# Two-layer graph kernel, first edge pass: ScalarE copies the sum of a group after the scaled relus of the next group of its batch

## The chip, the cores and the metric

The kernel runs on one core of a Trainium2 chip. The time is device time in microseconds (us) of one execution; a run's figure is a median over several executions. The engines named below are TensorE (PE, its weight loads PEld), VectorE (DVE), ScalarE (ACT), GpSimd (POOL) and SyncE (SP). Each runs its own queue of instructions in order; they wait for each other through semaphores. DMA transfers are issued from the queues of SP, ACT and POOL; all gathers of table rows by index are issued by POOL.

## What is computed

A graph with 30000 nodes of 128 features and 960000 edges sorted by destination. Layer 0 is two relational graph convolutions in a row, layer 1 is a gated convolution.

```python
def _rel_graph_conv(h, basis, coeff, bias, src, dst, etype, norm):
    W = jnp.einsum('rb,bdf->rdf', coeff, basis)          # 32 relations, 8 bases
    Hr = jnp.einsum('nd,rdf->nrf', h, W)
    msg = Hr[src, etype] * norm
    agg = jax.ops.segment_sum(msg, dst, num_segments=N)
    return agg + bias
...
h = jnp.maximum(_layernorm(x, axis=-1), 0.0)
x = x + layer0(h, ...)        # relu between its two convolutions
h = jnp.maximum(_layernorm(x, axis=-1), 0.0)
x = x + layer1(h, ...)        # sigmoid(k[dst] + q[src]) * v[src], summed by dst, mean of 4 types
```

## The kernel before

The edges are cut into tiles of 128 edges, three tiles make a group (384 edges, all of whose destinations lie in a window of 32 nodes), and five groups make a step. There are 2500 groups and 500 steps. Three edge passes follow each other: the first relational convolution, the second, and the gated layer. Each pass walks over all groups. A running sum `agg` (128 features by all nodes) stays in on-chip memory.

The change touches the body of the relational passes, and there only the order in the first one. What a step s of the first pass does, group by group (g = 0 to 4):

- POOL gathers the rows of x of the group's three tiles, three `DMA_INDIRECT` instructions (L118) into one buffer `hg` of a pool of seven. A gather into a buffer waits until the matmuls of the group that used it seven groups earlier are done.
- DVE takes the layer norm's statistics of the three gathered tiles (L410). Groups are normalised in two batches, which `BATCHES = {1: (0, 1), 4: (2, 3, 4)}` names: when group 1 has arrived, groups 0 and 1, and when group 4 has arrived, groups 2, 3 and 4. For a batch DVE combines the statistics (L415 to L420), ACT takes the square root (L422), DVE the reciprocal and the offset (L427, L429).
- DVE builds `sb` (L548): for each edge of the group its 8 basis coefficients, placed at its destination within the window.
- For each group of the batch ACT then runs three scaled relus in place on `hg` (L560), one for each tile; PE sums over the edges in `product`, three matmuls with 256 columns into a PSUM tile `pa` of a pool of three (L520), each of which waits for its own tile's relu; and ACT copies `pa` into `ab` (L531).
- After group 1, PE multiplies the previous step's `ab` by the eight bases into `pb` (`bases_out`, L478). PE then runs four small matmuls for the coefficients of a later step (L447), and in every second step two transposes that belong to finished nodes (L695, L696).
- At group 3, DVE adds the windows of an earlier step from `pb` into `agg` (`sums`, L351, five additions). They wait for the last `bases_out`, which writes the same PSUM tile. DVE's queue has them ahead of the statistics of group 4.

The order is written out by hand (`manual_schedule`): instructions stand in each engine's queue in the order in which the Python code makes them. In this pass the copy of a group stood at the end of `product`, so ACT's queue within a batch read: three relus, copy, three relus, copy, and in the longer batch once more. Between batches ACT also has the square roots, the copies and stores of finished nodes (L690, L699, L703) and the store of the coefficients for the second pass (L467).

The second pass runs the same code without statistics and relus and copies each group right after its product; the third pass has code of its own.

Of the kernel before, what the change touches and what calls it, by code (L numbers as in the profile page):

```python
# [72 lines left out]
def kernel(  # L73
# [43 lines left out]
    def gather(to, table, idx):  # L117
        return nc.gpsimd.indirect_dma_start(  # L118
            out=to, out_offset=None, in_=table,
            in_offset=bass.IndirectOffsetOnAxis(ap=idx, axis=0))  # L120
# [110 lines left out]
    def sorted_path():  # L231
# [7 lines left out]
        with ExitStack() as all_:  # L239
# [113 lines left out]
            def rel_body(table, weights, second):  # L353
# [21 lines left out]
                def body(bas, pos, hits, i, io, pool, ps, cp, iw, ic, beside):  # L375
# [5 lines left out]
                    def loads(k):  # L381
                        stage[k] = [stage_tile(io, "idx", src, I32, i, k)]
                        if second:
                            stage[k] += [stage_tile(io, "relc", reld, BF16, i, k),
                                         firsts(io, i, k)]
                        else:
                            dch = stage_tile(io, "dch", dst, I32, i, k)
                            fi = io.tile([TP, NGS], I32, name="fi")
                            n = i * NG + k * NGS
                            nc.sync.dma_start(fi, rows_of(first[n:n + NGS], TP))  # L390
                            stage[k] += [(dch, fi), firsts(io, i, k),
                                         stage_tile(io, "nrm", norm, F32, i, k,
                                                    4 * TQ - S * G)]

                    def positions(k):
                        dch, fi = stage[k][1]
                        relc = io.tile([TP, NTS], BF16, name="relc")
                        nc.vector.tensor_tensor(
                            relc.rearrange("p (g j) -> p g j", j=G),
                            dch.rearrange("p (g j) -> p g j", j=G),  # L400
                            fi.unsqueeze(2).to_broadcast([TP, NGS, G]), ALU.subtract)
                        stage[k][1] = relc
                        n = i * NQ + k
                        nc.scalar.dma_start(reld[:, n * NTS:(n + 1) * NTS], relc)
                        nc.vector.tensor_reduce(lo[:, n:n + 1], relc, AX.X, ALU.min)
                        nc.vector.tensor_reduce(hi[:, n:n + 1], relc, AX.X, ALU.max)

                    def statistics(st, hg):
                        for j in range(G):
                            nc.vector.bn_stats(st[:, j, :], hg[:, j, :])  # L410
# [86 lines left out]
                    for s in range(NS):  # L497
                        k = s // SB
                        if s % SB == 0:
                            if k + 1 < NQ:  # L500
                                loads(k + 1)
                        idx, relc, start = stage[k][:3]
                        if s + 2 < NS:
                            (kept if second else types)(s + 2)
                        z = s // A
                        if s % A == 0:
                            ab[z] = pool.tile([P, B, Z, W], F32, name="ab")
                        t0 = s % SB * S * G
                        nc.vector.tensor_tensor(
                            hits, iw[:TP].unsqueeze(1).to_broadcast([TP, S * G, W]),  # L510
                            relc[:, t0:t0 + S * G].unsqueeze(2).to_broadcast([TP, S * G, W]),
                            ALU.is_equal)
                        if not second and s % SB == SB - 1 and k + 1 < NQ:
                            positions(k + 1)
                        held = {}

                        def product(g, hg, rows, sb):
                            pa = ps.tile([P, B, W], F32, name="pa", bufs=3)
                            for j in range(G):
                                made = nc.tensor.matmul(  # L520
                                    pa.rearrange("p b w -> p (b w)"), lhsT=hg[:, j, :],
                                    rhs=sb[:, j].rearrange("p b w -> p (b w)"),
                                    start=(j == 0), stop=(j == G - 1))
                                if j == 0 and second:
                                    for other in rows[1:]:
                                        tc.add_manual_dep(
                                            made.ins, other.ins.name,
                                            mybir.DependencyInfo(mybir.DependencyClass.Sync,
                                                                 mybir.DependencyReason.DATA),
                                            reason="all rows of a group first")  # L530
                            nc.scalar.copy(ab[z][:, :, s % A * S + g, :], pa)  # L531

                        for g in range(S):
                            t0 = (s % SB * S + g) * G
                            hg = pool.tile([TP, G, D], F32, name="hg", bufs=5 if second else 7)
                            rows = [gather(hg[:, j, :], table, idx[:, t0 + j:t0 + j + 1])
                                    for j in range(G)]
                            ready = BATCHES.get(g)
                            if not second:
                                if g in (0, 2):  # L540
                                    st = pool.tile([TP, 3 * G, 6], F32, name="st")
                                at = (g if g < 2 else g - 2) * G
                                statistics(st[:, at:at + G], hg)
                                if ready:
                                    both, rs = spread(st, at + G)
                            sb = pool.tile([TP, G, B, W], F32, name="sb", bufs=4)
                            of = slice(g * G, (g + 1) * G)
                            nc.vector.tensor_mul(  # L548
                                sb, hits[:, of, :].unsqueeze(2).to_broadcast([TP, G, B, W]),
                                ce[s][:, of, :].unsqueeze(3).to_broadcast([TP, G, B, W]))  # L550
                            held[g] = hg, rows, sb
                            if second:
                                product(g, *held[g])
                            elif ready:
                                off = shifted(both, rs, at + G)
                                for q, one in enumerate(ready):
                                    for j in range(G):
                                        n = q * G + j
                                        mine = held[one][0][:, j, :]
                                        nc.scalar.activation(mine, mine, AF.Relu,  # L560
                                                             scale=rs[:, n:n + 1],
                                                             bias=off[:, n:n + 1])
                                    product(one, *held[one])
                            if g == 1 and z and s % A == 0:
                                bases_out(z - 1)
                            if g == 2 and not second and s + 1 < NS:
                                coefficients(s + 1)
                            if g == 3 and not second:
                                keep(s)
                                if s + 2 < NS:  # L570
                                    onehot(s + 2)
                            if second and z and s % 2 and g in (1, 3):
                                sums(s - 3 + g // 2)
                            if not second and g == 3 and s > 1:
                                sums(s - 2)
                            if s == NS - 1 and g == 2 and second:
                                bases_out(NS // A - 1, 0)
                            if s == NS - 1 and g == 4:
                                sums(NS - 2)
                            if g == 3 and s % SB == 1:  # L580
                                base[k] = bases(start, DVE)
                            beside(s * S + g)
# [552 lines left out]
```

## Time and profile before

| what | value |
|---|---|
| median of 10 runs | 36218.07 us (36176.04 to 36253.35) |
| the profiled execution's own time | 36205.21 us |
| its span | 36203.3 us |
| TensorE's mean granted clock in it | 0.663 |
| busy: PE, PEld | 21389.7 us (59%), 16826.8 us (46%) |
| busy: POOL | 21247.4 us (59%) |
| busy: DVE | 13768.0 us (38%) |
| busy: ACT | 6808.2 us (19%) |
| HBM traffic | 2603.78 MB read, 256.02 MB written |

Times on the page are microseconds unless marked ns. A row of a group of instructions names the line, the engine, the operation, the tile written and the tiles read, the count, then the busy time and the mean duration in ns, then how long the engine sat idle just before these instructions and what ended most of that idle time ("issue": nothing that the profile shows; "remote": a semaphore was raised by something that the profile can't name). In the timeline each row is a start, a duration, the engine and the instruction, with the idle time before it in brackets. The granted clock is TensorE's share of full speed: 1.0 or 0.5 at any moment, and a mean over a stretch.

No engine is busy for more than 59% of the span, and the span splits by pass: the first lasts to about 14160 us, the second to about 24890 us, the third to the end. In the stretch from 40 to 14180 us PE is busy for 7897.22 us, DVE for 5892.23, ACT for 4324.49 and POOL for 7072.25 us, at a granted clock of 0.68.

### The profile page before, as it was taken

How to read it: one execution, taken by the hardware profiler on the slowest of the kernel's cores; microseconds unless marked ns; L12 is line 12 of the kernel's file. 1: busy time of each engine (PE TensorE's matmuls, PEld its weight loads, DVE VectorE, ACT ScalarE, POOL GpSimd, SP SyncE). 2: the span in 40 equal slices, each digit the busy share in tenths (PEclk: the TensorE clock that was granted, in tenths of full speed). 3: DMA queues.
4: the chain of work that ended last, by engine and by line, in shares of the span. 5: the costliest groups of instructions: out<-in, count | busy, mean ns of one | idle time of the engine just before them, and what ended most of it. 6: DMA issues, size and time to landing. Idle time of an engine off the chain costs nothing. (4 is left out here: it accounts for less than half of the span.)

```text
span 36203.3 us, 289281 instructions
## 1 busy us (share of the span) xinstructions
PE 21389.7 (59%) x79371; PEld 16826.8 (46%) x79371; DVE 13768.0 (38%) x36932; ACT 6808.2 (19%) x18026; POOL 21247.4 (59%) x22513
## 2 busy tenths in 40 slices
PE   5555555555555556666666666666555655555565
PEld 3344444434444444444444444444555555555555
DVE  4444444444444443333333333333333333333333
ACT  3333323333333332111111111111111111111111
POOL 5445445445545445666666666666666666666666
PEclk7666666666666666778888788886555555555555
DMA  2112112112212212222222222223444444444444
GB/s 59 50 50 58 49 49 58 50 49 56 52 50 56 51 50 53 67 67 67 67 67 67 66 68 67 67 67 97 127 126 126 126 126 126 126 126 126 126 126 122
DMA packets 2002776, 2880.25 MB, mean 80 GB/s; under 512 B 708374, under 2 KB 1391247, under 8 KB 2001167
## 3 DMA queue, kind: packets, MB, share of 16 engines
q0 software_dynamic: 840000, 1967.52, 20.2%
q1 hardware_dynamic: 749240, 638.42, 6.1%
q10 hardware_dynamic: 411927, 255.71, 2.7%
q8 instruction: 662, 10.85, 0.1%
q14 instruction: 947, 7.76, 0.1%
HBM read 2603.78 MB, written 256.02 MB: 79 GB/s over the span
## 5 line engine op out<-in xcount | busy, mean ns | idle before, releaser
L520 PE MATMUL pa<-sb,hg 128*128 128x256 f32 x30000 | 10718.9, 514 | 8362.7 <-ACT hg L560 5080.0
L520 PEld LDWEIGHTS pa<-sb,hg 128*128 128x128 f32 x30000 | 7235.7, 256 | 11601.9 <-ACT hg L560 6101.5
L118 POOL DMA_INDIRECT hg<-in_x,idx x7500 | 7081.3, 944 | 7034.4 <-PE pa L520 4792.5
L118 POOL DMA_INDIRECT qv<-qvtab,qi x7500 | 7088.7, 945 | 4208.8 <-issue 2093.4
L118 POOL DMA_INDIRECT hg<-h,idx x7500 | 7075.4, 943 | 3647.9 <-issue 2125.6
L633 PE MATMUL po<-sel,msg 128*128 128x32 f32 x15000 | 3454.7, 386 | 4547.7 <-DVE msg L631 4163.6
L633 PEld LDWEIGHTS po<-sel,msg 128*128 128x128 f32 x15000 | 3427.9, 328 | 4835.3 <-DVE msg L631 4312.6
L531 ACT COPY ab<-pa 128x256 f32<-128x256 f32 x5000 | 1848.2, 373 | 14169.4 <-PE pa L520 6391.9
L659 DVE TENSOR_TENSOR pk<-pk,qv 128x384 f32<-128x384 f32 x2500 | 1405.8, 562 | 7001.4 <-remote 5534.1
L622 PE MATMUL pk<-kw,oh 128*128 128x128 f32 x15000 | 3997.2, 439 | 11.6 <-DMA kw<-ktab 11.6
L622 PEld LDWEIGHTS pk<-kw,oh 128*128 128x128 f32 x15000 | 3476.6, 331 | 11.8 <-issue 11.8
L560 ACT ACTIVATE hg<-hg,off,rs 128x128 f32<-128x128 f32 x7500 | 3155.3, 485 | 656.6 <-DVE off L429 491.0
L478 PE MATMUL pb<-ab,bas 128*128 128x160 f32 (+1 forms) x12080 | 2629.0, 376 | 406.9 <-issue 205.6
L351 DVE TENSOR_TENSOR agg<-agg,pb 128x32 f32 x5000 | 936.3, 187 | 4611.7 <-remote 3543.3
L660 ACT ACTIVATE pk<-pk 128x384 f32<-128x384 f32 x2500 | 1187.5, 475 | 7797.0 <-DVE pk L659 4720.0
L478 PEld LDWEIGHTS pb<-ab,bas 128*128 128x128 f32 x12080 | 2171.2, 214 | 876.2 <-issue 376.9
L548 DVE TENSOR_TENSOR sb<-cp,ce 128x768 f32<-128x768 f32 x2500 | 2319.5, 948 | 624.2 <-remote 423.5
L548 DVE TENSOR_TENSOR sb<-hits,ce 128x768 f32<-128x768 f32 x2500 | 2362.5, 945 | 59.3 <-PE pa L520 52.6
L410 DVE BATCH_NORM_STATS2 st<-hg 128x6 f32<-128x128 f32 x7500 | 1674.7, 278 | 167.3 <-issue 167.1
L427 DVE RECIPROCAL rs<-rs 128x6 f32<-128x6 f32 x1000 | 197.9, 198 | 3305.6 <-ACT rs L422 1206.4
L750 PE MATMUL bank<-wall,hT 128*120 128x512 f32 x1518 | 927.9, 728 | 746.8 <-ACT hT L746 316.0
L631 DVE TENSOR_TENSOR msg<-pk,qv 128x384 f32<-128x384 f32 x2500 | 1365.8, 546 | 0.0
(86 smaller groups left out, 7978.4 us busy)
## 6 DMA issues: line engine op xcount, KB each, us to landing
kb<-kcode SPq DMA_DIRECT2D x500, 480.0 KB
kw<-ktab SPq DMA_DIRECT2D x2500, 64.0 KB
er<-in_et_row SPq DMA_DIRECT2D x500, 256.0 KB
hg<-in_x,idx POOLq DMA_INDIRECT x7500
hg<-h,idx POOLq DMA_INDIRECT x7500
qvtab<-qvt ACTq DMA_DIRECT2D x250, 480.0 KB
qv<-qvtab,qi POOLq DMA_INDIRECT x7500
ktab<-kt ACTq DMA_DIRECT2D x253, 240.0 KB
```

The lines of the kernel that those rows point to most:

```text
L118: return nc.gpsimd.indirect_dma_start(out=to, out_offset=None, in_=table, in_offset=bass.IndirectOffsetOnAxis(ap=idx, axis=0))
L410: nc.vector.bn_stats(st[:, j, :], hg[:, j, :])
L478: nc.tensor.matmul(po[z][:, of].rearrange("p s w -> p (s w)"), lhsT=bas[:, b, :], rhs=ab[z][:, b, of].rearrange("p s w -> p (s w)"), start ...
L520: made = nc.tensor.matmul(pa.rearrange("p b w -> p (b w)"), lhsT=hg[:, j, :], rhs=sb[:, j].rearrange("p b w -> p (b w)"), start=(j == 0), ...
L531: nc.scalar.copy(ab[z][:, :, s % A * S + g, :], pa)
L548: nc.vector.tensor_mul(sb, hits[:, of, :].unsqueeze(2).to_broadcast([TP, G, B, W]), ce[s][:, of, :].unsqueeze(3).to_broadcast([TP, G, B, W]))
L560: nc.scalar.activation(mine, mine, AF.Relu, scale=rs[:, n:n + 1], bias=off[:, n:n + 1])
L622: nc.tensor.matmul(pk[n][:, j, :], lhsT=oh[n // S][:, n % S, j * TP:(j + 1) * TP], rhs=kw[n], start=True, stop=True)
L631: nc.vector.tensor_mul(msg, pk[n], qv[n][:, :, 1, :])
L633: nc.tensor.matmul(po[s][:, g, :], lhsT=msg[:, j, :], rhs=sel[s][:, g * G + j, :], start=(j == 0), stop=(j == G - 1))
L659: nc.vector.tensor_add(pk[n], pk[n], qv[n][:, :, 0, :])
L660: nc.scalar.activation(pk[n], pk[n], AF.Sigmoid)
```

## The change

The copy is taken out of `product`, which now returns its PSUM tile, and a new function `copied` issues it. The second pass calls it right after `product`, as before. In the first pass the copy of a group is issued after the relus and the product of the next group of the batch, and the copy of the batch's last group at the end. ACT's queue in the batch (0, 1) becomes: relus of 0, relus of 1, copy of 0, copy of 1. In the batch (2, 3, 4): relus of 2, relus of 3, copy of 2, relus of 4, copy of 3, copy of 4. Apart from a few separate wait instructions every engine issues the same work as before, and only ACT issues it in another order.

```diff
@@ in body, second and first pass
                                             reason="all rows of a group first")
-                            nc.scalar.copy(ab[z][:, :, s % A * S + g, :], pa)
+                            return pa
+
+                        def copied(g, pa):
+                            nc.scalar.copy(ab[z][:, :, s % A * S + g, :], pa)
...
                             if second:
-                                product(g, *held[g])
+                                copied(g, product(g, *held[g]))
                             elif ready:
...
                                         nc.scalar.activation(mine, mine, AF.Relu,
                                                              scale=rs[:, n:n + 1],
                                                              bias=off[:, n:n + 1])
-                                    product(one, *held[one])
+                                    made = product(one, *held[one])
+                                    if q:
+                                        copied(*last)
+                                    last = one, made
+                                copied(*last)
```

## The prediction

> **What bounds the kernel now.** I first asked which engine is full. None is: the page gives POOL and PE 59% each. So I took the pass that the change touches, the first, and read there who waits for whom (the list of waits of the stretch from 2000 to 12000 us, about 355 of the 500 steps; columns: waiter, releaser, us in total, times, longest).
>
> ```profile
> POOL hg L118 <- PE pa L520: 3393.3, 952, 12.4
> ...
> DVE agg L351 <- remote: 2482.2, 250, 12.5
> ...
> DVE agg L351 <- PE pb L478: 404.2, 66, 7.4
> ```
>
> POOL waits for buffers that PE frees: 3393.3 us over 355 steps, 9.6 us a step, nearly all in one long wait. DVE's additions L351 wait too: 250 times for a semaphore whose raiser the profile can't name, 66 times for PE's `pb`. How these belong together is seen in the timeline. Here are two steps in a row.
>
> ```profile
> 6003.13 2.93 PE L520 MATMUL pa<-sb,hg 128*128 128x256 f32 x6 [5.19 <-ACT hg L560]
> ...
> 6006.34 0.94 POOL L118 DMA_INDIRECT hg<-in_x,idx  x1 [8.69 <-PE pa L520]
> ...
> 6016.32 2.34 PE L478 MATMUL pb<-ab,bas 128*128 128x160 f32 x16
> ...
> 6023.97 0.95 POOL L118 DMA_INDIRECT hg<-in_x,idx  x1 [0.30 <-issue]
> ...
> 6027.91 1.08 DVE L351 TENSOR_TENSOR agg<-agg,pb 128x32 f32 x5 [10.92 <-remote]
> 6028.91 0.67 DVE L410 BATCH_NORM_STATS2 st<-hg 128x6 f32<-128x128 f32 x3
> ...
> 6031.51 1.26 ACT L560 ACTIVATE hg<-hg,off,rs 128x128 f32<-128x128 f32 x3 [0.83 <-DVE off L429]
> ...
> 6035.26 0.94 POOL L118 DMA_INDIRECT hg<-in_x,idx  x1 [10.34 <-PE pa L520]
> ...
> 6035.84 2.93 PE L520 MATMUL pa<-sb,hg 128*128 128x256 f32 x6 [0.85 <-ACT hg L560]
> ...
> 6043.55 0.30 ACT L422 ACTIVATE rs<-both,eps 128x6 f32<-128x6 f32 x1 [0.42 <-issue]
> ...
> 6044.85 2.93 PE L520 MATMUL pa<-sb,hg 128*128 128x256 f32 x6 [2.30 <-ACT rs L422]
> ...
> 6048.06 0.94 POOL L118 DMA_INDIRECT hg<-in_x,idx  x1 [1.79 <-issue]
> ...
> 6051.35 3.69 PE L478 MATMUL pb<-ab,bas 128*128 128x160 f32 x16
> ...
> 6055.31 1.08 DVE L351 TENSOR_TENSOR agg<-agg,pb 128x32 f32 x5 [7.37 <-PE pb L478]
> ...
> 6062.66 0.94 POOL L118 DMA_INDIRECT hg<-in_x,idx  x1 [7.39 <-PE pa L520]
> ```
>
> A step is a closed loop. POOL is released by the product of group 2 (6006.34) and issues a burst of fifteen gathers. Then it must wait for the next step's product of group 2. That one needs the statistics of group 4, and those stand in DVE's queue behind L351. From L351 to the next burst is a fixed tail: 6027.91 to 6035.26 and 6055.31 to 6062.66, 7.35 us both times. So the period is the time from the burst's first gather to L351, plus 7.35: 21.57 + 7.35 = 28.92 in the first step, 20.05 + 7.35 = 27.40 in the second.
>
> The odd thing is what ends the wait of L351. In the first step `pb` is finished by its records at 6018.66, yet L351 starts at 6027.91, 9.25 us later and 2.99 us after the last gather's end. In the second, PE is slower (matmuls of 2.93 where others take 1.56), `pb` ends at 6055.04, and L351 follows 0.27 us behind. The step in which PE was late is the shorter one. I took both marks from the timeline for all 495 steps with complete neighbours and sorted them by how long the tenth gather of the burst was held up (the one at 6048.06, which needs the product of group 0):
>
> - held up by 1.3 us or more: 139 steps, mean period 25.98 us, L351 in the median 19.7 us after the burst's start
> - less: 356 steps, mean 29.16 us, L351 at 21.5 us. Among them 202 with no hold-up at all (under 0.15 us): mean 29.14 us, L351 between 21.1 and 21.6 us nine times in ten, whether `pb` ended 12.3 or 16 us after the burst's start
> - all: 28.26 us, times 500 = 14130 us, the length of the pass.
>
> I can't name the mechanism; as a rule of this trace: a `pb` that ends early is seen by DVE only when the burst is over and 2 to 3 us more; a `pb` that ends 17 us or later after the burst's start is mostly seen soon. The fast steps are those in which PE is late.
>
> **The change, part by part.** *Relus move ahead of copies.* Before, product 3 waits for relus that wait for the copy of 2: PE stands idle 0.85 us between two products of a batch (row 6035.84). After, the relus of group 3 end 2 x 1.26 = 2.5 us after the first relu of group 2, while product 2 takes 2.93, so product 3 follows at once. In the batch of three two gaps of 0.85 vanish: 1.7 us earlier end of product 4. In the batch of two one gap: 0.85. *Copies move back.* The copy of 2 (0.37) comes up to 1.3 us later, those of 3 and 4 earlier. A product needs the copy of three groups before (three `pa` tiles); product 0 of the next step needs that of group 2, over by then: nothing, hidden behind products 3 and 4. Without that cover it would be one copy, 0.37 us a batch. *What stands behind on ACT.* L422 of the next batch comes behind the copy of 4: 1.7 us earlier, so product 0 starts at 6043.15 in place of 6044.85, and the tenth gather, held up 1.49 beyond the usual 0.30, is no longer held up. Stores and the two transposes' relu move forward with it. *Tail.* Product 2, which frees the next burst, has its relus first in both orders: 7.35 us stay. No instruction, DMA or byte is added.
>
> So PE ends `pb` at least 1.7 + 0.85 = 2.55 us earlier, and bursts run without the hold-up. By the rows, that takes the 139 short steps into the class of the 202. The price: bounds are 0 (they stay short) and 139 x (29.14 - 25.98) = 439 us. The 202 hold somewhat many of the steps with the longer tail of 9.2 us (48 of 202; all: 101 of 495), 0.04 x 1.85 = 0.07 us, and their steps with the earliest `pb` have L351 at 21.2 in place of 21.5. I put the new mean at 29.0 us: (29.0 - 28.26) x 500 = +370 us. On the profiled execution's 36205.2 (span 36203.3 and 1.9 around it; 13 below the median, which I neglect) that is 36575 us. Upper end: every step at 21.6 + 7.35 + 0.2 x 1.85 = 29.32, +530, 36735. Lower end of this case: half the short steps survive, +185, 36390. The second pass and the third keep their order: 0.
>
> The granted clock comes in: 0.68 in this pass, as PE falls to half speed in its idle stretches. Closing the gaps makes the stretch of three products 8.8 us without a break, so it may turn fast sooner, which moves `pb` still further into the class where nothing is gained. The Trainium skill, "TensorE: Matmul & The Clock Gate", Part 1, says that about 3.4 us of sustained activity release the half clock. By that page alone the third product and all behind it would take 1.56 in place of 2.93, and if `pb` set L351, as an estimate 3 x 1.37 us more would come off in each of the 139 steps, some 570 us in all. By the rows of the 202 steps it is worth nothing.
>
> **Rivals.** *L351 follows `pb` (faster).* If the short steps are short for another reason, and there `pb` goes on setting L351, each gains 2.55 us: 139 x 2.55 = 355, 35850 us; with half of them 36030. For it: the 66 waits that name `pb`. Against it: in 250 others an earlier `pb` brought nothing. It decides from the point where L351 starts less than 21 us after the burst's start though the tenth gather isn't held up. *No change.* The short steps' early release hangs on something that the order doesn't touch, and PE's gain lies in the wait of L351 as it does in the 250: 36205, within 70. For it: steps that alternate, the second kind (with the two transposes) being long whatever PE does. Against: among the others, the steps without the transposes, 116 (of 244) without a hold-up of 1.3 us have a mean of 29.15. *The order does not take effect,* since a copy held back blocks a `pa` tile: excluded by the three tiles, as above; it would show as a wait of L520 for the copy and give 36205 plus at most 0.37 x 1000 = 36575.
>
> **How the numbers follow.** Longer steps, 36390 to 36735: 0.68, likeliest 36575. Faster rival: 0.21. No change: 0.09, copies that block: 0.02 (slower). A measurement of this kernel tells 0.2% (72 us) from nothing. So faster 0.21, same 0.09, slower 0.70. The range goes from 36050, which takes in no change and the weakest part of the faster rival, to 36740.
>
> **What would show it.** Right: products of a batch without the 0.85 us in front; the tenth gather held up in few steps; L351's waits named "remote" near 500 for the pass and those for `pb` almost gone; the pass some 370 us longer, the tail still 7.35 us; passes two and three as they were. Wrong: L351 earlier than 21 us in many steps with an unbroken burst, or a pass of under 14100 us.

## The result, and the profile after

The changed kernel takes 36438.62 us (8 runs, 36427.5 to 36445.99) where the kernel before took 36223.49 (28 runs, 36176.04 to 36262.96): a ratio of 1.0059, 95% interval 1.0051 to 1.0068. It is slower by 215 us; the forecast was 357 us (36575 against 36218). The profiled execution has a span of 36443.5 us, 240 more than before (the two profiled executions lie 18 us below and 7 above the medians).

That is one kind of chip. Later runs fell on chips on which the kernel before takes 30528 to 30544 us, and there the same change is faster by 7.4% (run a2 below). Each later run is compared with the kernel before, timed beside it on the same chip; the text names the chips by that time, "36.2 ms chip" and "30.5 ms chips".

Where did the 240 us of span come from? The last gather of the first pass ends at 14376.6 us, before at 14117.9: 259 us later. From there to the end it is 22066.9 us, before 22085.4. So it is the first pass alone: a mean step of 28.79 us in place of 28.26. The waits of the stretch from 2000 to 12000 us, as shown of before (waiter, releaser, us in total, times, longest):

```profile
DVE agg L351 <- remote: 4340.0, 340, 14.5
POOL hg L118 <- PE pa L520: 3598.0, 526, 13.5
```

In some 347 steps L351 now waits 340 times for a raise of a semaphore that the profile can't name, 12.8 us each (before 250 times, 9.9 us). The line that named `pb` L478 as its releaser is gone. One step in the timeline (start, duration, engine and instruction, idle time before it):

```profile
3003.57 6.51 PE L520 MATMUL pa<-sb,hg 128*128 128x256 f32 x18 [15.10 <-ACT hg L563]
...
3006.53 0.37 ACT L534 COPY ab<-pa 128x256 f32<-128x256 f32 x1 [1.09 <-PE pa L520]
...
3006.77 0.94 POOL L118 DMA_INDIRECT hg<-in_x,idx  x1 [10.26 <-PE pa L520]
...
3011.91 2.86 PE L520 MATMUL pa<-sb,hg 128*128 128x256 f32 x12 [1.83 <-issue]
...
3014.60 2.34 PE L478 MATMUL pb<-ab,bas 128*128 128x160 f32 x16
...
3018.01 0.94 POOL L118 DMA_INDIRECT hg<-in_x,idx  x1 [0.30 <-issue]
...
3024.26 0.94 POOL L118 DMA_INDIRECT hg<-in_x,idx  x1 [0.30 <-issue]
3028.01 1.08 DVE L351 TENSOR_TENSOR agg<-agg,pb 128x32 f32 x5 [13.01 <-remote]
```

The products of a batch are now one row: 18 matmuls without a gap, then 12. The tenth gather (3018.01) starts 0.30 us behind the ninth, so the burst runs unbroken in 18.42 us. `pb` is written by 3016.94 in the records. Yet L351 starts at 3028.01, 11 us later and 2.8 us after the end of the last gather (3025.20). PE's semaphore shows it directly: its raises for `pb`, for L447 and for the two transposes, which the records end between 3016.94 and 3017.99, all come between 3027.92 and 3028.08. Over the stretch from 100 to 8000 us the lateness builds up within a burst: of the 784 matmuls that make a raise and end in a burst's first 2 us, 781 have one recorded within 0.15 us, of those that end 6 to 8 us into it 28 in 100, of those at 10 to 12 us 2 in 100; between bursts (26 to 28 us) all 431 have one. The raises of DVE and ACT aren't late here: none of 7765 and 4388 comes 1 us behind its instruction. Over 495 steps L351 starts 21.2 us after the burst's start (21.1 to 21.5 in eight steps of ten), while `pb` ends at 10.3 in the median (before at 16.4).

### The profile page after: what moved, and what is told of

It is laid out like the page before. It is cut to its first block, busy times and chain, and to the rows that moved or that the text cites. A ratio compares the mean times of both kernels' runs of the same rounds, so it can differ in the third digit from the quotient of the medians.

```text
span 36443.5 us, 289276 instructions
## 1 busy us (share of the span) xinstructions
PE 19842.9 (54%) x79371; PEld 16404.8 (45%) x79371; DVE 13772.8 (38%) x36932; ACT 6749.4 (19%) x18026; POOL 21267.6 (58%) x22513
## 5 line engine op out<-in xcount | busy, mean ns | idle before, releaser
L520 PE MATMUL pa<-sb,hg 128*128 128x256 f32 x30000 | 9307.8, 471 | 10131.0 <-ACT hg L563 7338.1
L520 PEld LDWEIGHTS pa<-sb,hg 128*128 128x128 f32 x30000 | 6971.6, 241 | 12267.0 <-ACT hg L563 7503.5
L351 DVE TENSOR_TENSOR agg<-agg,pb 128x32 f32 x5000 | 936.4, 187 | 6438.4 <-remote 6236.0
L563 ACT ACTIVATE hg<-hg,off,rs 128x128 f32<-128x128 f32 x7500 | 3047.3, 482 | 659.8 <-DVE off L429 526.0
L478 PE MATMUL pb<-ab,bas 128*128 128x160 f32 (+1 forms) x12080 | 2476.3, 360 | 322.3 <-ACT ab L534 198.4
L478 PEld LDWEIGHTS pb<-ab,bas 128*128 128x128 f32 x12080 | 2009.1, 199 | 757.4 <-issue 274.5
L422 ACT ACTIVATE rs<-both,eps 128x6 f32<-128x6 f32 x1000 | 301.9, 302 | 7317.6 <-DVE both L420 7156.4
L740 DVE BATCH_NORM_STATS2 st<-bank 120x6 f32<-120x128 f32 x253 | 75.5, 299 | 3303.8 <-remote 1862.3
```

The costliest lines, as they stand in the source:

```text
L478: nc.tensor.matmul(po[z][:, of].rearrange("p s w -> p (s w)"), lhsT=bas[:, b, :], rhs=ab[z][:, b, of].rearrange("p s w -> p (s w)"), start ...
L520: made = nc.tensor.matmul(pa.rearrange("p b w -> p (b w)"), lhsT=hg[:, j, :], rhs=sb[:, j].rearrange("p b w -> p (b w)"), start=(j == 0), ...
L563: nc.scalar.activation(mine, mine, AF.Relu, scale=rs[:, n:n + 1], bias=off[:, n:n + 1])
```

## The experiments

**Loop or not: the additions moved.** First I tested that the step's loop runs through L351 at all. In e1 the changed kernel issues the additions two groups earlier, ahead of the `bases_out` that writes their tile; e2 does the same to the kernel before. Both on the 36.2 ms chip.

```diff
+                            if not second and g == 1 and s > 1:
+                                sums(s - 2)
                             if g == 1 and z and s % A == 0:
                                 bases_out(z - 1)
...
-                            if not second and g == 3 and s > 1:
-                                sums(s - 2)
```

> The additions L351 of step s-2 are issued at group 1, ahead of the bases_out of step s-1, so that they need only the bases_out of the step before. Theory A (the step's loop runs through L351, which waits for a semaphore of PE that is raised late; the burst of gathers, 18.4 us, is then the next bound): the first pass falls from 28.8 us a step to between 19 and 25 us, 500 x (28.8 - 19 to 25) = 1900 to 4900 us, a total of 31500 to 34500. Rival B (another wait for the same late semaphore, the one-hot sums of the next step, hits L509, which wait for L447, takes its place in DVE's queue): 28 to 29 us a step, total 36100 to 36500.

> The same early additions with the copies in the order of before. Theory A: L351 out of the loop, the order of the copies still costs 1.7 us in the chain from the statistics to product 0 and 0.85 us between products, so this is equal to e1_sums_early where POOL is the bound, or up to 500 x 2.5 = 1250 us slower than it; the order of the change is then the better one. Rival B (the loop goes on through a late semaphore): this one stays ahead of e1_sums_early by 200 to 250 us, as before is ahead of the changed kernel.

e1: 33012.21 us, ratio 0.9113 (0.9098 to 0.9128), 21.9 us a step. e2: 33092.08, ratio 0.9135 (0.912 to 0.9151). Theory A holds for both, and rival B of either run is out: over 3100 us were the price of one wait, in either order of the copies. With L351 out of the loop the change is worth 80 us on this chip too, where alone it loses 215. The waits of e1 (2000 to 10000 us):

```profile
ACT ab L534 <- remote: 1299.0, 241, 8.9
...
DVE agg L707 <- remote: 1070.8, 127, 11.2
DVE hits L509 <- remote: 768.5, 92, 10.6
...
POOL hg L118 <- remote: 623.4, 189, 3.7
```

L351 no longer has a line of size. Raises that nobody can be named for now hold the copies, the finished nodes (L707), the one-hot sums and POOL itself. POOL's waits for these and for products (716.1 us on L520) come to 3.7 us a step, and a step takes 21.9 us in place of the 18.7 of fifteen gathers.

**PE made late by work.** The prediction had read that the short steps are those in which PE is late. So I made PE late, on the same chip.

```diff
                             if g == 1 and z and s % A == 0:
-                                bases_out(z - 1)
+                                for _ in range(1 if second else 4):
+                                    bases_out(z - 1)
```

> The changed kernel with bases_out done four times in a row in each step of the first pass (the same result each time), 3 x 2.34 = 7.0 us of PE work more in each step. Theory A (steps are short when PE ends pb late, whatever held it up): pb ends about 11.0 + 7.0 = 18.0 us after the start of the burst, L351 follows at once in the steps without transposes (243 of 489), which become 18.1 + 7.7 = 25.8 us, and perhaps in the others: total 36440 - 700 to 1500 = 34900 to 35750, faster with more work. Rival B (before's short steps were short because the burst itself had a hole at the tenth gather): L351 stays at 21.2 us, total 36440 within 70. Rival C (PE's work counts): 7 us more in each step, total up to 39900.

38929.8 us, ratio 1.0746 (1.0728 to 1.0764): 5.0 us a step slower than the changed kernel. Theory A falls, and so does rival B, which had the time unchanged; rival C, that PE's work counts, comes nearest (5.0 us of its 7). The timeline of the burst that begins at 3004.22 and whose last gather ends at 3022.66 shows more:

```profile
3011.99 5.20 PE L478 MATMUL pb<-ab,bas 128*128 128x160 f32 x36
...
3018.30 0.43 PE L478 MATMUL pb<-ab,bas 128*128 128x160 f32 x2 [1.10 <-issue]
...
3020.39 0.43 PE L478 MATMUL pb<-ab,bas 128*128 128x160 f32 x1 [1.67 <-issue]
...
3021.11 0.90 PE L478 MATMUL pb<-ab,bas 128*128 128x160 f32 x2 [0.29 <-issue]
...
3023.22 0.43 PE L478 MATMUL pb<-ab,bas 128*128 128x160 f32 x1 [1.21 <-issue]
...
3025.35 5.02 PE L478 MATMUL pb<-ab,bas 128*128 128x160 f32 x19 [0.26 <-issue]
...
3030.48 1.07 DVE L351 TENSOR_TENSOR agg<-agg,pb 128x32 f32 x5 [18.09 <-PE pb L478]
```

36 matmul records follow each other in 5.2 us, the next nine take from 3018.30 to 3025.09, and at 3025.35, again 2.7 us after the last gather's end, PE runs on at its pace. So it is not only the raise that is late: here PE's work itself comes almost to a halt until the gathers are over. The Trainium skill, "TensorE: Matmul & The Clock Gate", "Architectural detail", gives TensorE's queue 64 entries. 36 matmuls with their weight loads are 72 instructions; whether a full queue is what stops PE, no run here shows.

**A pause in the burst, by a wait.** In e4 the last three gathers of a burst wait for the `bases_out` of the step before.

```diff
+                            if not second and g == 3 and s:
+                                tc.add_manual_dep(
+                                    rows[0].ins, ab["made"].ins.name,
...
```

> The changed kernel with the gathers of group 3 of each step (the last three of a burst) made to wait for the bases_out of the step before, so that POOL pauses after twelve gathers until PE's semaphore is raised. Theory A (the raise comes some 2.7 us after POOL has gone quiet, and not at a fixed time): POOL's twelfth gather ends 14.6 us after the burst's start, the raise comes at about 17.4, L351 starts there, next burst 7.4 us later: 25 us a step, total about 34500 (34000 to 35200). Rival (the raise comes at a fixed time of the step, 21.2 us, whatever POOL does): POOL pauses until then, L351 stays at 21.2, and the three last gathers follow beside the tail: total 36440 within 100. A third (the raise waits for the landing of the whole burst for another reason): POOL pauses longer than 10 us, total above 36600.

37240.95 us, ratio 1.0281 (1.0263 to 1.0298): the third case by its time, but the timeline shows the pause longer for another reason.

```profile
3019.24 0.95 POOL L118 DMA_INDIRECT hg<-in_x,idx  x1 [0.30 <-issue]
...
3022.67 0.37 ACT L535 COPY ab<-pa 128x256 f32<-128x256 f32 x1 [3.50 <-remote]
...
3029.32 2.34 PE L478 MATMUL pb<-ab,bas 128*128 128x160 f32 x16
...
3032.42 0.95 POOL L118 DMA_INDIRECT hg<-in_x,idx  x1 [12.24 <-issue]
```

POOL is quiet from 3020.19. The raise that the copy waits for comes 2.4 us later; what follows (square root, relus, two products, `pb`) then takes until 3031.66 with every raise in time. So the raises come out once POOL is quiet, but the awaited `pb` had not even begun; the edit put a chain of 9 us into the loop. It settles nothing on the size of the gain.

**The parts of the change, and holes of fixed length.** The next runs fell on a 30.5 ms chip, which I had not reckoned with. e5 keeps the new order in the batch of three alone, e6 in the batch of two alone; e7 and e7s put memsets on POOL ahead of the tenth gather.

```diff
 e5 (e6: the other way round)
+                                    if len(ready) != 3:
+                                        copied(one, made)
+                                        continue
...
 e7 (e7s: once)
+                            if not second and g == 2:
+                                idle = pool.tile([TP, 1024], F32, name="idle", bufs=1)
+                                for _ in range(3):
+                                    nc.gpsimd.memset(idle, 0.0)
```

> The change in the batch of three alone (relus of 2, 3, copy of 2, relus of 4, copies of 3, 4); the batch of two as before. L422 and product 0 come 1.7 us earlier, so the tenth gather isn't held up; pb 1.7 us earlier. Theory H (what made before's short steps short is the hole in the burst, the tenth gather held up by 1.3 us or more): nearly all steps long, like the changed kernel: 36350 to 36500. Rival P (it is the time at which PE ends pb): pb ends about 15.4 us after the burst's start in the steps that had it at 17.1, also all long: the same. Both fall if this kernel stays at 36220; then it is the batch of two that costs.

> The change in the batch of two alone (relus of 0, 1, copies of 0, 1); the batch of three as before, so the tenth gather stays held up by 1.49 us where it was, and pb ends 0.85 us earlier. Theory H (the hole in the burst makes the short steps): about as many short steps as before, 36150 to 36300. Rival P (the time at which PE ends pb decides): pb at 16.3 in place of 17.1 us after the burst's start falls among the steps with L351 at 21.2, long: 36380 to 36500.

> The changed kernel with three memsets of 128x1024 on POOL before the tenth gather of each burst: a hole of some 3 us (the trace will tell) in which POOL issues no gather; all else as in the changed kernel, pb done by the records 11 us after the burst's start. Theory H (a pause of POOL lets PE's late semaphores out): L351 starts at about 14 us, the next burst follows when POOL is done with this one, some 22 us a step, total about 33000 (32500 to 34500): idling POOL makes the kernel faster. Rival P (the raise is late when PE is early, whatever POOL does): L351 stays at the burst's end plus 2.7, which moves by the hole: 36440 + 500 x 3 = 37900.

> The same with one memset, a hole of some 1 us, less than the 1.49 us by which before's short steps held the tenth gather up. Theory H, if a short pause is enough: as many or more short steps than before, below 36220. Theory H, if the pause must last as long as the time from a burst's end to L351 (2.7 us): 36440 + 500 x 1 = 36940. Rival P: 36940 too.

| run | time, us | before on this chip | ratio (interval) | mean step, first pass |
|---|---|---|---|---|
| e5, batch of three | 28501.03 | 30543.62 | 0.9334 (0.9317 to 0.9352) | 19.39 us |
| e6, batch of two | 29987.58 | 30543.62 | 0.9823 (0.9804 to 0.9841) | 22.36 us |
| e7, hole of 2.84 us | 29675.01 | 30543.62 | 0.972 (0.9699 to 0.9742) | 21.74 us |
| e7s, hole of 0.83 us | 28652.89 | 30543.62 | 0.9386 (0.9365 to 0.9407) | 19.69 us |

All four expectations were stated for the other kind of chip, and none can be judged by its times; e5, e6 and e7s weren't run on that kind, so theory H for the parts of the change and for a short hole stays untested there. What the traces show instead is why this chip is faster. I compared the raises of PE's semaphore recorded from 100 to 8000 us with the end of PE's latest matmul that makes one: in the kernel before on the 36.2 ms chip 20% come over 1 us late, in the changed kernel 23%, in e1 52%. (The expectation of a2 below has 36 and more; these counts don't give that for the first two.) In these four runs none of 6351 to 7339 does. The traces differ in the number of raises too: the changed kernel's has 3731 for 4932 matmuls that make one, e5's 7339 for 7341, so the shares on the first chip hold only for the raises that are recorded. The gathers are alike on both (0.94 us, 0.30 us apart), and so are the DMA packets of 4096 bytes that they move (median 201 ns before, 202 in e5, over the whole execution). The other two passes gain too, 22085 us there and 18818 us here (e6), with the code untouched.

**The change where nothing is late.** So the changed kernel was run once more, with e8 beside it: e1 in which the one-hot sums read their index row from SBUF rather than from the PSUM tile that L447 writes.

```diff
+                    iw = iw if second else irow
```

> The changed kernel once more, since the kernel before took 36223 us on the chip of the first runs and 30544 us on that of e5 to e7s, where no raise of PE's semaphore in the trace is over 1 us late (36 in 100 and more were around there). Theory L (the loss comes from PE's late raises alone, and these belong to the chip): where the kernel before takes about 30540, this takes what e5_late_in_three took or less, 28150 to 28510, ratio 0.92 to 0.935; where it takes about 36220, it takes 36440 again, ratio 1.006. Rival (the change costs by itself, whatever the raises do): a ratio over 1 on both kinds of chip.

> e1_sums_early, and in the first pass the one-hot sums L509 read the index row from SBUF and not from the PSUM tile that L447 writes, so that they wait for no raise of PE. Theory A (each wait of DVE for a late raise adds to the loop): where the kernel before takes about 36220, less than the 33012 of e1_sums_early, 31500 to 32900. Rival (POOL's wait for product or the copies' waits set the pace there): 33012 within 100. Where the kernel before takes about 30540, POOL's gathers are the bound at 18.72 us a step, and it is equal to the changed kernel on that chip within 150 us, 28100 to 28500.

It fell on a chip of the second kind. The changed kernel: 28235.89 us against 30527.86, ratio 0.9257 (0.9236 to 0.9277). e8: 28287.4, ratio 0.9273 (0.9252 to 0.9293), 51 us behind it. Theory L holds: no raise of 7512 is late, and the sign turns. The timeline and the waits (2000 to 9000 us) of the changed kernel there:

```profile
3000.53 2.34 PE L478 MATMUL pb<-ab,bas 128*128 128x160 f32 x16
...
3002.97 1.08 DVE L351 TENSOR_TENSOR agg<-agg,pb 128x32 f32 x5 [1.34 <-PE pb L478]
```

```profile
DVE agg L351 <- PE pb L478: 492.3, 278, 3.7
POOL hg L118 <- PE pa L520: 165.6, 523, 2.3
```

L351 follows `pb` by 0.1 us in the midst of the gathers, nothing is "remote", and POOL waits for products 165.6 us in some 370 steps, 0.45 us a step. A step is 18.86 us, fifteen gathers at 1.248 are 18.72: POOL is the bound. For the kernel before on this chip I have no trace; 30527.86 less the 18802 that the other passes take (28233.5 - 9431.8, the end of the first pass in a2) leaves 11726 us, 23.4 us a step. So what the change removes is worth 4.6 us a step there, and e5 and e6 say in which batch: the batch of three alone brings 2043 us, the batch of two alone 556. The holes of e7 and e7s cost there what they last: 29675 - 28236 = 1439 us, 2.88 us a step, and 417, 0.83 a step (across two chips whose kernel before differs by 16 us).

**The hole and the row again.** The last two runs are e8 and e7 once more, on a chip of the first kind (the kernel before 36637.96 us).

> The same kernel as e8_own_index_row, for a chip on which PE's raises are late. Where the kernel before takes about 36220: theory A (each of DVE's waits for a late raise adds to the loop) 31500 to 32900; rival (the copies' and POOL's own waits for late raises set the pace, 21.9 us a step in e1_sums_early) 33012 within 100. Where it takes about 30530: 28290 within 50 again.

> The same kernel as e7_hole_three_memsets, for a chip on which PE's raises are late; its hole is 2.84 us beyond the usual 0.30. Where the kernel before takes about 36220: theory H (a pause of POOL lets PE's late raises out) L351 at about 14 us after the burst's start, 21.7 us a step as where nothing is late, the first pass 10900 us, total 32500 to 34500; rival P (raises come 2.7 us after the last gather of a burst, whatever pause it had) L351 at 24, 31.6 us a step, total about 37900. Where it takes about 30530: 29675 within 50 again.

e7b: 33626.07 us, ratio 0.9179 (0.9164 to 0.9194). With POOL kept from gathering for 3 us in each step the changed kernel is 8% faster than the kernel before where raises are late, as theory H had it (32500 to 34500), and the rival's 37900 is out; without the hole it was 0.6% slower than before on the 36.2 ms chip (it wasn't run on this one). L351 moves to 14.3 us after the burst's start in the median, a step takes 22.7 us. In the timeline:

```profile
3028.30 2.34 PE L478 MATMUL pb<-ab,bas 128*128 128x160 f32 x16
...
3030.38 0.95 POOL L118 DMA_INDIRECT hg<-in_x,idx  x1 [0.31 <-issue]
...
3031.32 3.00 POOL L542 MEMSET idle<- 128x1024 f32 x3
...
3033.41 1.08 DVE L351 TENSOR_TENSOR agg<-agg,pb 128x32 f32 x5 [4.71 <-remote]
...
3034.47 0.95 POOL L118 DMA_INDIRECT hg<-in_x,idx  x1 [0.15 <-issue]
```

`pb` ends by its records at 3030.64, POOL's last gather before the hole at 3031.33, and the raises of `pb`, L447 and the transposes come together from 3033.32 to 3033.48, 2.0 us into the hole. The memsets keep POOL busy all that time: the raises wait for a pause in the gathers, not in POOL's work as such.

e8b: 33343.23 us, ratio 0.9102 (0.9087 to 0.9117), against 0.9113 (0.9098 to 0.9128) for e1: the same, by ratios, as the kernel before differs by 1.1% between the two. The rival holds; one DVE wait less brings nothing that can be measured.

## Why the prediction was right, and where it wasn't

*Products close up, the tenth gather runs free.* As forecast: one row for a batch, and the tenth gather held up by 1.3 us or more in 3 of 489 steps, before in 139 of 495. In those three L351 still starts early, 10.6 us after the burst's start in the median.

*`pb` earlier, L351 not.* Forecast was `pb` at least 2.55 us earlier with nothing gained. It ends at 10.3 us after the burst's start, 6.1 us earlier in the median, since PE also turns to full speed. The windows of the changed kernel's trace (from and to, length, then busy times and counts of PE, PEld, DVE, ACT and POOL, the granted clock, DMA share and GB/s):

```profile
3003.60:3008.40 4.80, 4.80 (x11) 3.84 (x12) 3.95 (x15) 3.37 (x9) 1.32 (x2) 0.50 0.00 0
3008.40:3018.00 9.60, 7.76 (x46) 6.64 (x44) 4.04 (x13) 4.38 (x12) 7.18 (x8) 1.00 0.32 74
```

In this step the clock doubles after 4.8 us of unbroken work; over 358 such starts up to 9000 us it takes 2.8 to 6.2 us, 4.3 in the median, where the rule weighed in the prediction says about 3.4; the choice between the two sums there, nothing or 570 us, went the trace's way on this chip.

*The tail* is 7.35 us in the median, as forecast, and the other passes kept their length (18 us less).

*The price* is the term that was mis-sized. The prediction put the new mean step at 29.0 us; it is 28.79, so (28.79 - 28.26) x 500 = 265 in place of 370 us. With unbroken bursts L351 starts at 21.2 us, where I had kept near the 21.5 that most of the earlier long steps showed. (A small slip in the same sum: 48 of 202 against 101 of 495 is 0.034, not 0.04, worth 0.06 us and not 0.07.)

*The mark of a short step* was read wrongly in one sentence: "The fast steps are those in which PE is late." e3 made PE late and lost 5 us a step. The trace of before would have told: of its steps in which `pb` ends 17 us or later, the 129 with the tenth gather held up have L351 at 19.4 us in the median, the 72 without at 21.5. What made steps short is the hole in the burst, which the sorting had used as its mark; the number came from that and not from the sentence. e7b shows the same with a hole made by memsets.

*The faster rival* had its condition named: L351 under 21 us with the tenth gather not held up. On the 30.5 ms chips it is met in nearly every step (in a2, where the gathers run on without a break, L351 starts 4.5 us in the median after the gather that began a burst on the other chip), and the price is 2292 us rather than 355, because the loop through L351 opens altogether. The chances of 0.70 and 0.21 were given from one trace of one chip, which can't show that the lateness goes with the chip. The forecast came true on the kind of chip that its trace was taken on; on the other kind its sign would have been wrong.

*What stays open:* why raises are late on some chips, and by which path gathers hold them. From 100 to 8000 us 96 in 100 of the changed kernel's 854 late raises stand outside the gathers, mostly 2.5 to 3.0 us after the end of the last one, and in e4 99 in 100, mostly at 2.3 to 2.6 us; in e7b 31 in 100 come between gathers, so a pause is not the whole condition. The raise being late rather than PE's work is argued from four raises within 0.16 us for work that the records spread over 1 us. But the profile only models the end of a matmul, and e3 shows that PE stalls as well. The record numbers the chips: 0 in e1 to e4, e7b and e8b, 4 in e5 to e7s, 9 in a2 and e8. Raises are late on number 0 alone, but the kernel before takes 36223 us there in the first of these and 36638 in the last, so a chip's state may matter beside the chip. Every execution timed here was also recorded, and the traces of the late kind hold far fewer semaphore events, for the landings of DMAs 99168 in the changed kernel against 461566 in a2; whether the recording has a part in the lateness, no run here tells.

## What to carry to other kernels

Where an engine waits long for work that the records show as long done, look at the raises of that semaphore before costing anything, and ask for a second chip: the same reordering was 0.6% slower on one and 7.4% faster on another. A wait on a false dependency, here additions that share a PSUM tile with the next step's result, is best taken out by issuing the reader ahead of the next writer: worth 9% where raises are late (e1), and 51 us behind the best where they are not (e8, which also reads its own index row; e1 itself wasn't run there). That makes e1's place for the additions, with the new order of copies, the version to keep.

## What the hardware did that I had not expected

- On chips where the kernel before takes 36.2 to 36.6 ms, PE's semaphore is raised up to 11.8 us (changed kernel) after the recorded end of the latest matmul while POOL issues gathers one behind the other, mostly 2 to 3 us after the last of them; DVE's and ACT's are in time in that trace (in e1 4% of DVE's are over 1 us late). On others, none of some 7000 raises of PE is 1 us late. Gathers and their packets take the same time on both.
- Three memsets of 128x1024 on POOL (3.00 us) in the midst of the gathers go with a step of 22.7 us on such a chip (28.8 us without them, on the 36.2 ms chip), and cost 2.88 us a step on the 30.5 ms chips.
- PE's own records stall as well: nine matmuls in 6.8 us behind the first 36 in e3.
